# GpSimd in written order through the first tiles, and the side work of a factorization rearranged

## The chip, the cores and the metric

The program runs on one core of a Trainium2 chip. The metric is the device time of one execution in microseconds (us). Five engines run side by side and meet only at semaphores: TensorE (PE, with its weight loads shown as PEld), VectorE (DVE), ScalarE (ACT), GpSimd (POOL) and SyncE (SP), which issues the DMAs. A run has the time of the whole execution; the profile of one execution has a span, from its first to its last instruction.

## The reference

The function is a rotation of the tokens in a 64-dimensional subspace, followed by one transformer block that is modulated by a condition. All data are float32; 8 sequences of 512 tokens with 576 features.

```python
U, _ = jnp.linalg.qr(P)                      # P is 576 x 64
v = silu(cond) @ W.T + b                     # 8 x 2016
A = zeros(8, 64, 64).at[:, iu, ju].set(v).at[:, ju, iu].set(-v)
R = expm(A)                                  # 8 rotations, 64 x 64
z = x @ U
x = x + (z @ R - z) @ U.T

ada = silu(cond) @ ada_w + ada_b             # 8 x 3456, six parts of 576
shift_a, scale_a, gate_a, shift_m, scale_m, gate_m = split(ada, 6)
x = x + gate_a * attention(modulate(layernorm(x), shift_a, scale_a))
x = x + gate_m * mlp(modulate(layernorm(x), shift_m, scale_m))
```

The attention is between the 16 heads of one token, not between tokens: per token a 16 x 16 softmax over heads of 36 features. The MLP has 2304 hidden features and an exact GELU.

## The kernel before

The kernel has a preparation (lines 150 to 679) and a main part (from line 681).

**Preparation.** A Householder QR of P runs in 64 written steps, `qr_step(j, ...)` at line 259. One step is a chain: two small matmuls on PE (`rp` at line 262, `dp` at line 270), some ten small DVE instructions, two ACT instructions, and the DVE products of the next column (`column_products`). Beside it the generator `beside` (line 497) hands out work, one piece a step, called by `next(side, None)` after step j from j = 2 on. Its pieces are, in order:

- `ada_columns(g)`, nine groups of 384 columns of the modulation, each five PE products (line 352) accumulated in PSUM; six of the groups first, four products a step;
- `skew_entries(g)`, eight groups of the entries of A, five products of 252 columns each (line 385), four a step; then `skew_rows` sends them through DRAM into the tile `au`;
- `modulation(v)`, ten tiny transposing matmuls (line 363) that turn a row of `ada` into the per-feature tile `mod`, interleaved with single products of the last three `ada` groups;
- `expm`, the exponential: au is masked on POOL, powers by `products` (line 409, sixteen 64 x 64 matmuls a call), a polynomial whose sums run on POOL (lines 442 to 463), and 19 squarings with two POOL additions each (line 493). A `yield True` leaves room for one more piece from `rest` in that step, a `yield False` does not.

After step 63 a tail (lines 548 to 679) inverts a triangular matrix by doubling, level by level (lines 595 to 607), and builds `gz`, `u` and `ut`, with which the tokens are rotated; `normed` (line 130) prepares the layer norm of the first tile: two statistics on DVE, then the power -1/2 on POOL (line 140), then the scaling on DVE (line 141).

PE, DVE and ACT are in `tc.manual_schedule` during the preparation: their instructions run in the written order. POOL and SP are not in it before the change. For an engine outside of it a planner simulates the program and places instructions when they are ready in its simulation, with written order as the priority. In the main part all engines are planned this way.

**Main part.** Tokens go in tiles of 128. `rotation(b)` gives six pieces (project to z, rotate two tiles, and so again), `feature_major` (line 748) transposes normed tiles and applies `mod`, `qkv(b, i)` makes the attention inputs of a tile in four groups of ten PE matmuls, `attention(b, ts)` is DVE work of some sixteen 2.55 us instructions a tile. The work order is `units` (line 1081): the first two tiles alone (units 0 and 1, with `mlp_plain`), then pairs of tiles (with `mlp`). `mlp` computes the second layer by a seven-product scheme of 2 x 2 blocks that needs sums of weight blocks. `next_sums` (line 949), called ten times, makes them: call g first stores the sums of call g-1 to `comb_d` (SP, line 953), then loads block g into a tile `tt` (line 957, in a ring of three buffers shared with a part of the projection weights), and makes four sums on POOL (lines 960 to 963). Until the pairs begin, all nine sets must be made.

`mlp_plain` streams both MLP weights from HBM for one tile: `w1` (line 923, ring of four) and `w2` (line 980, ring of three).

Of the kernel before, what the change touches and what calls it, by code (L numbers as in the profile page):

```python
# [18 lines left out]
R = 64  # L19
# [29 lines left out]
def rotate_then_dit_block(  # L49
# [53 lines left out]
    def srows(c):  # L103
        return 65 if c == 4 else 128
# [42 lines left out]
    normed_x = {}  # L147


    engines = {mybir.EngineType.PE, mybir.EngineType.DVE, mybir.EngineType.Activation}  # L150
    sc = const.tile([128, NK, B], F32, tag="sc", name="sc")
    with tc.manual_schedule(engines=engines), tc.tile_pool(name="prep", bufs=1) as prep, tc.tile_pool(name="qrs", bufs=2) as qrs, tc.tile_pool(
        name="ada", bufs=4
# [271 lines left out]
        def expm(i1, i2, half):  # L425
# [35 lines left out]
                    nc.gpsimd.tensor_tensor(acc, acc, tp, ALU.add)  # L461
            nc.gpsimd.tensor_scalar(nan, nan, 0.0, 3e38, ALU.is_gt, ALU.mult)
            nc.gpsimd.tensor_scalar(nan, nan, 3e38, 0.0, ALU.mult, ALU.mult)
            for _ in range(5):
                yield True
            for name in ("c", "n"):
                lo, hi, tp = parts[name]
# [26 lines left out]
                yield False  # L494
            nc.gpsimd.tensor_tensor(fmi, f, nan.unsqueeze(2).to_broadcast([128, B // 2, R]), ALU.add)

        def beside():
            yield
            yield
            yield from paced(4, [ada_columns(g) for g in range(6)])  # L500
            yield from paced(4, [skew_entries(g) for g in range(8)])
            skew_rows()
            rest = paced(1, [ada_columns(g) for g in range(6, 9)])
            for v in (0, 1, 3):
                modulation(v)
                next(rest)
                yield
            for free in expm(*eyes):
                if free:
                    next(rest, None)  # L510
                yield
            for _ in rest:
                yield
            modulation(4)
            yield

        for g in range(4):
            load_ada(g)
        for g in range(4):
            cols = slice(g * NSKEW // 4, (g + 1) * NSKEW // 4)  # L520
            load_rows(wr[:, :, cols], rot_w[:, cols], 65)
        for g in (4, 5):
            load_ada(g)
        block_masks()
        first_xT = xin.tile([128, NK, 256], F32, tag="xT", name="xT_0_0")
# [4 lines left out]
        for j in range(R):  # L530
            t, done = qr_step(j, t, done)
            if j > 1:
                next(side, None)
            if j == 30:
                nc.sync.dma_start(out=first_xT, in_=x_t[0, :, :, 0:256].rearrange("c p s -> p c s"))
                nc.sync.dma_start(out=first_xt, in_=x[0, 0:128, :])
            if j == 8:
                load_rows(wqkv, qkv_w, 65)
                nc.sync.dma_start(out=b2, in_=fc2_b.to_broadcast([128, D]))
                for g in (6, 7, 8):  # L540
                    load_ada(g)
        for _ in side:
            pass

# [3 lines left out]
        if True:  # L548
# [32 lines left out]
            nc.tensor.matmul(vf_ps, lhsT=m[0:R, 0, :], rhs=fmi[0:R, 0, :], start=True, stop=True)  # L581
            vf = square("vf")
            nc.scalar.copy(vf, vf_ps)
            xps = ps_m.tile([R, R], F32, tag="m", name="xps")
            nc.tensor.matmul(xps, lhsT=y_, rhs=ident[0:R, 0:R], start=True, stop=True)
            nc.vector.scalar_tensor_tensor(ls[2], vv, rd, lower[2], ALU.mult, ALU.mult)
# [4 lines left out]
            for c, rows in enumerate(KROWS):  # L591
                ps = ps_ex.tile([R, 128], F32, tag="ex", name=f"vt_{c}")
                nc.tensor.transpose(ps[:, 0:rows], m[0:rows, c, :], ident[0:rows, 0:rows])
                nc.scalar.copy(vt[:, c * 128 : c * 128 + rows], ps[:, 0:rows])
            for c, s in enumerate(LEVELS[1:]):
                p1 = ps_qr.tile([R, R], F32, tag="dp", name=f"p1_{s}")
                nc.tensor.matmul(p1, lhsT=ls[s], rhs=x_, start=True, stop=True)
                vx_chunk(c)
                p1s = qrs.tile([R, R], F32, tag="p1s", name=f"p1s_{s}")
                nc.vector.tensor_copy(p1s, p1)  # L600
                p2t = ps_m.tile([R, R], F32, tag="m", name=f"p2t_{s}")
                nc.tensor.matmul(p2t, lhsT=p1s, rhs=y_, start=True, stop=True)
                if s < LEVELS[-1]:
                    p2 = ps_m.tile([R, R], F32, tag="m", name=f"p2_{s}")
                    nc.tensor.matmul(p2, lhsT=y_, rhs=p1s, start=True, stop=True)
                    nc.vector.tensor_tensor(x_, x_, p2, ALU.subtract)
                nc.vector.tensor_tensor(y_, y_, p2t, ALU.subtract)

            vxs = prep.tile([R, 128], F32, tag="vxs", name="vxs")
            nc.scalar.copy(vxs, vx)  # L610

# [44 lines left out]
            for n in range(2):  # L656
                cols = slice(n * HALF, (n + 1) * HALF)
                ps = ps_qr.tile([128, HALF], F32, tag="rp", name=f"first_rot_{n}")
                nc.tensor.matmul(ps, lhsT=first_zT, rhs=gz[0:R, cols], start=True, stop=True)
                nc.vector.tensor_tensor(first_xt[:, cols], first_xt[:, cols], ps, ALU.add)  # L660
                for c in (2 * n, 2 * n + 1):
                    u_rows(c, KROWS[c])
            nc.sync.dma_start(out=xr_d[0][0:128, :], in_=first_xt)
            normed_x[0, 0] = [normed(first_xt, "a0_0")]
            u_rows(4, KROWS[4])
            nc.vector.tensor_tensor(u[0:R, 0, 0:R], u[0:R, 0, 0:R], ident[0:R, 0:R], ALU.add)
# [81 lines left out]
    def feature_major(b, half):  # L748

        if b not in hTs:  # L750
            hTs[b] = big.tile([128, NK, S], F32, tag="hT", name=f"hT_{b}")
        hT = hTs[b]

        pair = normed_x.pop((b, half))
        first = half * 256 + (256 - len(pair) * 128 if b == 0 and half == 0 and turned else 0)
        turned.add((b, half))
        tokens = slice(first, first + len(pair) * 128)
        for c in range(NK):
            rows = srows(c)
            ps = ps_mm.tile([128, 2, 128], F32, tag="mm", name=f"htr_{b}_{half}_{c}")  # L760
            for t in range(len(pair)):
                nc.tensor.transpose(ps[:, t, :], pair[t][:, c * 128 : (c + 1) * 128], ident)
            nc.scalar.activation(
                hT[0:rows, c, tokens],
                ps[0:rows].rearrange("p t s -> p (t s)")[:, 0 : len(pair) * 128],
                AF.Identity,
                bias=mod[0:rows, 0, c, b : b + 1],
                scale=mod[0:rows, 1, c, b : b + 1],
            )

    toks = {}

# [312 lines left out]
            piece()  # L1085

    first = rotation(0)
    now(first[:1])
    feature_major(0, 0)
    now(qkv(0, 0))  # L1090
    now(first[2:3])
    feature_major(0, 0)
    next_sums()
    now(first[3:])
    next_sums()
    now(qkv(0, 1))
    feature_major(0, 1)
    attention(0, (0,))
    next_sums()
    now(qkv(0, 2))  # L1100
    gate_a = gate_m = gb2 = None
    for k, (b, ts) in enumerate(units):
        if ts[0] == 0:
            gate_a, gate_m = gate_rows(0, b), gate_rows(1, b)
            gb2 = big.tile([128, D], F32, tag="gb2", name=f"gb2_{b}")
            nc.gpsimd.tensor_tensor(gb2, gate_m, b2, ALU.mult)

        pr = Projection(b, ts, gate_a)
        if k == 2:
            next_sums()  # L1110
        if k == 0:
            q = qkv(0, 3)
        elif k == 1 or k + 1 == len(units):
            q = []
        else:
            nb, nts = units[k + 1]
            q = qkv(nb, nts[0]) + qkv(nb, nts[1])
        if len(ts) == 1:
            now(q[:3])
            pr.turn(0)  # L1120
# [92 lines left out]
```

## Time and profile before

| | us |
|---|---|
| median of 3 runs | 2202.04 |
| lowest to highest | 2199.09 to 2203.98 |
| the profiled execution, as a run | 2199.16 |
| its span | 2197.1 |
| PE busy | 2094.7 |
| DVE busy | 1797.5 |
| POOL busy | 691.1 |

The difference of 2.06 us between run and span lies around the instructions. PE is busy 95% of the span; most of the 5% lies in the first 460 us, which are the preparation and the two single tiles. In the profile a row of the timeline has start, length, engine, line, operation, output and inputs, shapes, and the number of merged instructions; a float32 matmul appears as two records.

### The profile page before, as it was taken

What the parts mean: (1) busy time and instruction counts of PE and PEld (TensorE: products, weight loads), DVE (VectorE), ACT (ScalarE), POOL (GpSimd) and SP (SyncE); (2) the same over time, 40 slices, a digit from 0 to 9 for tenths busy, and PEclk for the clock granted to TensorE, in tenths of its full rate; (3) what the DMA queues carried; (4) which work ended last, traced back from release to release, by engine and by line L of the source; (5) the groups of instructions that cost most, each with busy time, mean ns of one, the idle gap of its engine ahead of it and who ended that gap; (6) DMA issues with size and microseconds to landing.
All of it is one profiled execution on the core that took longest, in us unless ns stands there. A gap on an engine that the chain in (4) does not pass through costs nothing.

```text
span 2197.1 us, 26306 instructions
## 1 busy us (share of the span) xinstructions
PE 2094.7 (95%) x9609; PEld 1567.4 (71%) x9609; DVE 1797.5 (82%) x2450; ACT 389.7 (18%) x831; POOL 691.1 (31%) x882
## 2 busy tenths in 40 slices
PE   7897788899999999999999999999999999999998
PEld 3467446767777777868686868777776868686877
DVE  8998399899986979888896979697978888797930
ACT  2223121121021112111111112111211122111110
POOL 2144301003333333423241424243332334142422
PEclk9755699999999999999999999999999999999999
DMA  9103326845756473827374556546473737373753
GB/s 306 58 2 113 105 80 183 271 152 149 218 173 185 134 200 129 238 92 214 110 246 125 173 156 200 160 154 180 161 225 98 220 112 213 105 217 110 215 172 122
DMA packets 214291, 355.55 MB, mean 162 GB/s; under 512 B 82670, under 2 KB 101563, under 8 KB 214164
## 3 DMA queue, kind: packets, MB, share of 16 engines
q1 hardware_dynamic: 214164, 353.88, 53.0%
q8 instruction: 77, 1.26, 0.2%
q14 instruction: 50, 0.41, 0.1%
HBM read 321.43 MB, written 32.39 MB: 161 GB/s over the span
## 4 chain that ended last, share of the span: by engine, by line
PE 56%; DVE 23%; issue 12%; DMA 5%; POOL 3%; ACT 1%; SPq 1%; POOLq 0%; DVEq 0%; ACTq 0%
PE fc L926 23%; PE fc L1032 7%; DVE pv L831 5%; PE qkvp L784 5%; PE fc L1037 5%; DVE att L837 4%; DVE sc L815 4%; DVE qk L809 2%; PE fc L1034 2%; PE p L1047 2%; PE zps L725 2%; DMA out<-x 1%; PE rot L733 1%; PE dp L270 1%; DMA gate<-gates_d 1%
## 5 line engine op out<-in xcount | busy, mean ns | idle before, releaser
L926 PE MATMUL fc<-h2T,w 128*128 128x256 f32 (+3 forms) x3060 | 657.5, 368 | 1.4 <-ACT h2T L902 1.3
L926 PEld LDWEIGHTS fc<-h2T,w 128*128 128x128 f32 (+1 forms) x3060 | 550.1, 191 | 75.4 <-ACT h2T L902 6.5
L784 PE MATMUL qkvp<-wqkv,hT 128*128 128x432 f32 (+1 forms) x1280 | 478.6, 527 | 1.8 <-DVE pt L883 1.1
L809 DVE TENSOR_TENSOR qk<-qkv 128x2304 f32<-128x2304 f32 x128 | 330.2, 2580 | 124.4 <-ACT qkv L791 121.9
L784 PEld LDWEIGHTS qkvp<-wqkv,hT 128*128 128x128 f32 (+1 forms) x1280 | 239.7, 190 | 204.2 <-issue 195.4
L831 DVE TENSOR_TENSOR pv<-sc,qkv 128x2304 f32<-128x2304 f32 x128 | 330.1, 2579 | 3.2
L837 DVE TENSOR_REDUCE att<-pv 128x144 f32<-128x2304 f32 x128 | 326.6, 2551 | 3.2
L815 DVE TENSOR_REDUCE sc<-qk 128x64 f32<-128x2304 f32 x128 | 326.4, 2550 | 2.9
L1017 POOL TENSOR_TENSOR ss<-gt 128x128 f32<-128x128 f32 x135 | 143.0, 1060 | 579.5 <-ACT gt L934 579.5
L934 ACT ACTIVATE gt<-fc 128x512 f32<-128x512 f32 (+1 forms) x153 | 87.5, 572 | 716.9 <-PE fc L926 716.7
L791 ACT COPY qkv<-qkvp 128x432 f32<-128x432 f32 x128 | 66.3, 518 | 546.0 <-PE qkvp L784 545.9
L1037 PEld LDWEIGHTS fc<-wt,ss 128*128 128x128 f32 x1080 | 150.5, 190 | 14.2
L1037 PE MATMUL fc<-wt,ss 128*128 128x144 f32 x1080 | 154.4, 286 | 0.0
L1032 PE MATMUL fc<-wq,gt 128*128 128x288 f32 x540 | 153.0, 405 | 0.0
L140 POOL TENSOR_TENSOR rstd_m<-rstd_m,mhalf 128x1 f32<-128x1 f32 x32 | 19.8, 618 | 337.2 <-DVE rstd_m L139 337.2
L1063 DVE TENSOR_TENSOR u<-u,fc 128x288 f32<-128x288 f32 x15 | 6.8, 454 | 135.0 <-ACT u L1062 135.0
L1032 PEld LDWEIGHTS fc<-wq,gt 128*128 128x128 f32 x540 | 100.8, 189 | 21.3
L942 POOL TENSOR_TENSOR x<-x,mt 128x288 f32<-128x288 f32 x64 | 53.0, 829 | 183.0 <-DVE mt L941 183.0
L881 PE MATMUL pj<-w2q_p,aT 128*128 128x288 f32 x384 | 105.5, 411 | 3.9 <-DVE pt L883 1.8
L1019 POOL TENSOR_TENSOR ss<-gt,ss 128x128 f32<-128x128 f32 x135 | 101.8, 754 | 10.6
L1020 POOL TENSOR_TENSOR s<-gt 128x128 f32<-128x128 f32 x135 | 92.9, 688 | 0.0
L881 PEld LDWEIGHTS pj<-w2q_p,aT 128*128 128x128 f32 x384 | 70.0, 189 | 30.5 <-issue 7.1
(255 smaller groups left out, 2356.6 us busy)
## 6 DMA issues: line engine op xcount, KB each, us to landing
w<-in_fc_w SPq DMA_DIRECT2D x306, 320.0 KB, 3.5
wt<-comb_d SPq DMA_DIRECT2D x135, 432.0 KB, 5.2
wq<-in_fc_q SPq DMA_DIRECT2D x135, 432.0 KB, 3.3
w2q_p<-in_proj_w SPq DMA_DIRECT2D x34, 432.0 KB, 4.4
w<-in_fc_w SPq DMA_DIRECT2D x36, 288.0 KB, 3.8
xT<-in_x_t SPq DMA_DIRECT2D x16, 640.0 KB, 7.2
w2t_p<-in_proj_w SPq DMA_DIRECT2D x34, 288.0 KB, 5.1
xt<-in_x SPq DMA_DIRECT2D x32, 288.0 KB, 5.3
```

Of the source, the lines that this page charges most:

```text
L784: nc.tensor.matmul(ps, lhsT=hT[0:k, c, i * 128 : (i + 1) * 128], rhs=wqkv[0:k, c, n * N : (n + 1) * N], start=c == 0, stop=c == NK - 1,)
L809: nc.vector.tensor_tensor(pr, q[:, c * HC : (c + 1) * HC].unsqueeze(2).to_broadcast([128, HC, H, DH]), k.unsqueeze(1).to_broadcast([128, H ...
L815: nc.vector.tensor_reduce(sc2[:, t, c * HC : (c + 1) * HC, :], pr, AX.X, ALU.add)
L831: nc.vector.tensor_tensor(pr, sc2[:, t, c * HC : (c + 1) * HC, :].unsqueeze(2).to_broadcast([128, HC, DH, H]), v.unsqueeze(1).to_broadcast ...
L837: nc.vector.tensor_reduce(att[:, c * HC : (c + 1) * HC, :], pr, AX.X, ALU.add)
L881: nc.tensor.matmul(ps, lhsT=aT[0:k, c, :], rhs=w, start=c == 0, stop=c == NK - 1)
L926: nc.tensor.matmul(ps[:, k], lhsT=w1[0:n, c, :], rhs=h2T[0:n, c, 0 : NU * 128], start=c == 0, stop=c == NK - 1,)
L1017: nc.gpsimd.tensor_tensor(ss[:, 0], gt[:, 0, 1], gt[:, 1, 1], ALU.add)
L1019: nc.gpsimd.tensor_tensor(ss[:, 2], gt[:, 1, 0], ss[:, 1], ALU.subtract)
L1020: nc.gpsimd.tensor_tensor(s3s[g], gt[:, 0, 0], gt[:, 0, 1], ALU.subtract)
L1032: nc.tensor.matmul(p[k], lhsT=whole[k][0], rhs=whole[k][1], start=g == 0, stop=stop)
L1037: nc.tensor.matmul(bank[:, side], lhsT=lhs, rhs=rhs[:, n * QUARTER : (n + 1) * QUARTER], start=False, stop=stop, skip_group_check=True,)
```

## The change

POOL joins the manual schedule of the preparation, and a second manual schedule holds POOL alone from the first rotation until unit 2 begins. In `beside` the skew entries come first, four products a step; then a new generator `modulations` gives all nine groups of `ada` and the four modulations, three items a step: four steps alone, then in the `True` steps of `expm`, which has one `yield True` less. Weights for the skew entries are loaded first, and those of `ada` group g + 4 when group g is done. In the tail the products `vx_chunk` move to another place in each level, `vxs` is copied earlier, and the addition of the identity to `u` comes inside the loop over n. `feature_major` transposes up to four chunks of a single tile into one PSUM buffer before ScalarE reads them. The calls of `next_sums` are placed anew: one after the six pieces of the first rotation, two after the first attention, one before the MLP of unit 0 and two in it (g = 2 and 6), one before the MLP of unit 1 and two in it (g = 0 and 6), and the last in unit 2. There are still ten.

```diff
-    engines = {mybir.EngineType.PE, mybir.EngineType.DVE, mybir.EngineType.Activation}
+    engines = {mybir.EngineType.PE, mybir.EngineType.DVE, mybir.EngineType.Activation, mybir.EngineType.Pool}
...
-            for _ in range(5):
+            for _ in range(4):
                 yield True
...
+        def modulations():
+            for g in range(9):
+                yield from ada_columns(g)
+                if g + 4 < 9:
+                    load_ada(g + 4)
+                v = {1: 0, 2: 1, 5: 3, 7: 4}.get(g)
+                if v is not None:
+                    modulation(v)
+                    yield
+
         def beside():
             yield
             yield
-            yield from paced(4, [ada_columns(g) for g in range(6)])
             yield from paced(4, [skew_entries(g) for g in range(8)])
             skew_rows()
-            rest = paced(1, [ada_columns(g) for g in range(6, 9)])
-            for v in (0, 1, 3):
-                modulation(v)
+            rest = paced(3, [modulations()])
+            for _ in range(4):
                 next(rest)
                 yield
             for free in expm(*eyes):
...
             for _ in rest:
                 yield
-            modulation(4)
-            yield
-
-        for g in range(4):
-            load_ada(g)
+
         for g in range(4):
             cols = slice(g * NSKEW // 4, (g + 1) * NSKEW // 4)
             load_rows(wr[:, :, cols], rot_w[:, cols], 65)
-        for g in (4, 5):
+        for g in range(4):
             load_ada(g)
...
-                for g in (6, 7, 8):
-                    load_ada(g)
...
+            vxs = prep.tile([R, 128], F32, tag="vxs", name="vxs")
...
-            for c, s in enumerate(LEVELS[1:]):
+            vx_chunk(0)
+            for c, s in enumerate(LEVELS[1:], 1):
                 p1 = ps_qr.tile([R, R], F32, tag="dp", name=f"p1_{s}")
                 nc.tensor.matmul(p1, lhsT=ls[s], rhs=x_, start=True, stop=True)
-                vx_chunk(c)
                 p1s = qrs.tile([R, R], F32, tag="p1s", name=f"p1s_{s}")
                 nc.vector.tensor_copy(p1s, p1)
+                if s == LEVELS[-1]:
+                    nc.scalar.copy(vxs, vx)
...
                     nc.tensor.matmul(p2, lhsT=y_, rhs=p1s, start=True, stop=True)
+                    vx_chunk(c)
                     nc.vector.tensor_tensor(x_, x_, p2, ALU.subtract)
...
                     u_rows(c, KROWS[c])
+                if n == 0:
+                    nc.vector.tensor_tensor(u[0:R, 0, 0:R], u[0:R, 0, 0:R], ident[0:R, 0:R], ALU.add)
             nc.sync.dma_start(out=xr_d[0][0:128, :], in_=first_xt)
             normed_x[0, 0] = [normed(first_xt, "a0_0")]
             u_rows(4, KROWS[4])
-            nc.vector.tensor_tensor(u[0:R, 0, 0:R], u[0:R, 0, 0:R], ident[0:R, 0:R], ALU.add)
...
-        for c in range(NK):
-            rows = srows(c)
-            ps = ps_mm.tile([128, 2, 128], F32, tag="mm", name=f"htr_{b}_{half}_{c}")
...
+        at_once = 4 if len(pair) == 1 else 1
+        for first_c in range(0, NK, at_once):
+            cs = range(first_c, min(first_c + at_once, NK))
+            ps = ps_mm.tile([128, 4, 128], F32, tag="mm", name=f"htr_{b}_{half}_{first_c}")
+            for c in cs:
+                for t in range(len(pair)):
+                    at = (c - first_c) * len(pair) + t
+                    nc.tensor.transpose(ps[:, at, :], pair[t][:, c * 128 : (c + 1) * 128], ident)
+            for c in cs:
...
     first = rotation(0)
+    in_order = ctx.enter_context(ExitStack())
+    in_order.enter_context(tc.manual_schedule(engines={mybir.EngineType.Pool}))
     now(first[:1])
     feature_major(0, 0)
     now(qkv(0, 0))
     now(first[2:3])
     feature_major(0, 0)
-    next_sums()
     now(first[3:])
     next_sums()
     now(qkv(0, 1))
     feature_major(0, 1)
     attention(0, (0,))
+    next_sums()
     next_sums()
...
         if k == 2:
+            in_order.close()
             next_sums()
...
         if k == 0:
-            aside = {g: next_sums for g in (1, 3, 5, 7)}
+            aside = {g: next_sums for g in (2, 6)}
+        if k == 1:
+            aside |= {0: next_sums, 6: next_sums}
```

More of the change, by code (lines that the diff above doesn't have):

```diff
@@ L605, in rotate_then_dit_block @@
                     nc.tensor.matmul(p2, lhsT=y_, rhs=p1s, start=True, stop=True)
+                    vx_chunk(c)
                     nc.vector.tensor_tensor(x_, x_, p2, ALU.subtract)
                 nc.vector.tensor_tensor(y_, y_, p2t, ALU.subtract)
-            vxs = prep.tile([R, 128], F32, tag="vxs", name="vxs")
-            nc.scalar.copy(vxs, vx)
             w1_ps = ps_m.tile([R, R], F32, tag="m", name="w1_ps")
@@ L757, in feature_major @@
         tokens = slice(first, first + len(pair) * 128)
-        for c in range(NK):
-            rows = srows(c)
-            ps = ps_mm.tile([128, 2, 128], F32, tag="mm", name=f"htr_{b}_{half}_{c}")
[L761 to L769, printed above, removed]
+        at_once = 4 if len(pair) == 1 else 1
[7 more added lines that the diff above has]
+            for c in cs:
+                rows = srows(c)
+                at = (c - first_c) * len(pair)
+                nc.scalar.activation(
+                    hT[0:rows, c, tokens],
+                    ps[0:rows, at : at + len(pair)].rearrange("p t s -> p (t s)"),
+                    AF.Identity,
+                    bias=mod[0:rows, 0, c, b : b + 1],
+                    scale=mod[0:rows, 1, c, b : b + 1],
+                )
     toks = {}
```

## The prediction

> **What bounds the kernel now.** I read the page first, then the busy time of the engines stage by stage, then the waits of PE, then the timeline around the few stages where PE is not full.
>
> ```profile
> span 2197.1 us, 26306 instructions
> PE 2094.7 (95%) x9609; PEld 1567.4 (71%) x9609; DVE 1797.5 (82%) x2450; ACT 389.7 (18%) x831; POOL 691.1 (31%) x882
> ...
> PE   7897788899999999999999999999999999999998
> ...
> PEclk9755699999999999999999999999999999999999
> ```
>
> PE is the bound from the ninth slice on. Before it PE is neither full nor at full clock: what can be won lies there.
>
> ```profile
> 139.86:195.22 55.36, 54.62 (x668) 50.81 (x669) 53.18 (x310) 21.82 (x74) 25.33 (x36) 0.50 0.01 2
> 242.78:289.13 46.35, 30.13 (x82) 16.91 (x83) 25.28 (x23) 8.06 (x17) 15.81 (x14) 0.73 0.36 122
> 353.17:460.00 106.83, 97.52 (x586) 81.02 (x587) 94.42 (x81) 22.47 (x44) 6.99 (x9) 0.98 0.88 268
> 460.00:2197.00 1737.00, 1713.60 (x7505) 1308.99 (x7504) 1413.54 (x1173) 286.07 (x523) 583.00 (x693) 1.00 0.55 166
> ```
>
> Columns: stretch and length, busy us of PE, PEld, DVE, ACT, POOL, granted clock, DMA share, GB/s. The 19 squarings (139.86 to 195.22) take 2.91 us a step. The first rotation (242.78 to 289.13) leaves PE idle for 16 us. The two single tiles (353 to 460) run the DMA engines at 88%. After 460 us PE is 98.7% busy and the change touches nothing, so what is won or lost before 460 is the result.
>
> ```profile
> PE over L453 <- POOL ns L442: 3.3, 1, 3.3
> ...
> PE htr L762 <- DVE xm L141: 14.1, 1, 14.1
> PE fc L989 <- DMA w<-in_fc_w: 6.2, 8, 1.9
> ...
> PE zps L725 <- DVE u L666: 2.0, 1, 2.0
> ```
>
> Three of these waits end at POOL, once by way of DVE: it was doing something less urgent.
>
> **The change part by part.** The starts of QR steps are those of `rp` (line 262) in the timeline of PE: step 4 at 20.57, 5 at 26.59, 14 at 56.66, 31 at 118.01, 38 at 139.86, 57 at 195.22, 63 at 212.93. Where PE is not late a step lasts what DVE needs (its floor): 3.31 at step 13, 3.12 at 20, 2.98 near 33, 2.31 at 62.
>
> ```profile
> 22.32 4.34 PE L352 MATMUL ada<-aw,sc 128*8 128x384 f32 x8
> 30.64 2.75 PE L352 MATMUL ada<-aw,sc 128*8 128x384 f32 x8
> 89.95 1.45 PE L352 MATMUL ada<-aw,sc 128*8 128x384 f32 x2
> ...
> 58.02 1.87 PE L385 MATMUL skew<-wr,sc 128*8 128x252 f32 x8
> ```
>
> Two records are one product: 0.69 us at full clock (2.75/4), 1.4 at half.
>
> *Step 4, skew first.* The first four products warm the clock. Four `ada` took 4.34: about 4.6 records at 0.69 and the rest at 0.34, so some 3.2 us cold. Four skew products by the same rule: 6.7 records at 0.47, the rest at 0.23, 3.45. **-0.9.** Their first quarter of weights, now first in SP's queue, has 17 us to land (1.1 MB at 340 GB/s: 3.4).
>
> *Steps 5 to 13.* Four `ada` (2.75) made these PE-bound: 30.07. Four skew (1.87) leave them DVE-bound, nine floors near 3.40: 30.6. **+0.5.**
>
> *Steps 14 to 30.* Before: 61.35, of which 2.8 are two cold steps with a modulation (22, 23), 1.6 two more late ones, 4.2 the wait of `over`. There POOL ran seven polynomial instructions ahead of the tiny `ns` (issued at 109.68, its input ready at 105.5). In written order `ns` comes first and that wait goes; then DVE's reduction (105.11) is what POOL awaits, and seventeen polynomial instructions of 0.8 (14 us) are queued behind it, due five steps (16 us) later, two of them moved here from the kernel's start. After: floors of 52.4 (17 steps, mean 3.08). PE has 0.35 + 0.35 + 2.07 for three products, 2.77, hidden under the floor; with a modulation (1.26 warm at 80.36) instead of a product, or powers (0.65), it is over the floor, by 0.1, 0.8, 0.3, 0.7, 0.35, 0.3 and 1.0 in seven steps: 3.5. Add 1.0 for skew DMAs that nine `t` loads on SP (line 958, 7.7 us of issue) may now delay. The clock: three products stream 2.07 in a step of 3.2, more than the 1.87 that kept full clock in steps 12 to 20. The Trainium skill ("TensorE: Matmul & The Clock Gate", "HAM oscillation") says that a PE gap of over 3.4 us re-throttles. Step 27 has no product, a gap of some 4.2 us with only 64 x 64 matmuls, which held no clock in the squarings. By the row nothing is lost; by the rule step 28 runs cold at 4.14 for its products, about +2.2. I take 1.5, since such small matmuls run without raising 0.50. Sum 58.4, **-3.0.**
>
> *Steps 31 to 62.* The squarings now sit at 31 to 49. Seven meet the floor of about 3.1, twelve keep 2.91: 56.6. Then thirteen steps have no side work but one `ada` product in step 50: mean floor 2.52, 32.8. I read that floor from steps 58 and 62 (2.60, 2.31), since 59 to 61 are stretched to 3.39 by the weight sums on POOL, as the squarings are by its additions:
>
> ```profile
> 176.03 0.67 DVE L299 TENSOR_TENSOR m<-m,dg 128x1 f32<-128x1 f32 x1
> ...
> 211.65 0.15 DVE L299 TENSOR_TENSOR m<-m,dg 128x1 f32<-128x1 f32 x1
> ```
>
> The same instruction, beside POOL and without it. 89.4 against 94.92: **-5.5.** The QR makes **-8.9**.
>
> *Tail.* One `vx` product, 0.62, goes in front of the levels; the four others leave the gap before `p2t` (0.2 each) for that before the next `p1` (0.2 each): **+0.4**. `u` is complete before `ut`, so `zps` starts at about 240.9 and not 242.78: **-1.9**. With POOL in written order the power at 241.11 no longer waits behind a memset that waited for `ut`; its scaling then ends in time for the transposes.
>
> *Transposes of a single tile.* From 244.84 to the first `qkvp` at 247.71 five transposes alternate with ScalarE. Four at once: 4 x 0.36, a step of ScalarE 0.46, and a hop: 2.05. **-0.8**, and **-0.6** at the second, followed by `zps`.
>
> *The power of the second tile.*
>
> ```profile
> 272.95 0.14 DVE L139 TENSOR_SCALAR rstd_a<-mv_a 128x1 f32<-128x1 f32 x1
> 273.55 2.98 POOL L961 TENSOR_TENSOR t<-tt,t 128x288 f32<-128x288 f32 x1
> 278.23 0.55 POOL L140 TENSOR_TENSOR rstd_a<-rstd_a,mhalf 128x1 f32<-128x1 f32 x1
> 278.82 0.58 DVE L141 TENSOR_SCALAR xm<-xt,mv_a,rstd_a 128x576 f32<-128x576 f32 x1 [2.93 <-POOL rstd_a L140]
> 279.45 0.69 PE L762 MATMUL htr<-ident,xm 128*128 128x128 f32 x2 [14.06 <-DVE xm L141]
> ```
>
> The power was ready at 273.09 and started 5.1 us later, behind sums. But DVE has a 2.8 us product from 273.07 to 275.88 in front of the scaling: that is late next. Only DVE's own wait of 2.93 goes: **-2.9**, not 14.1. At 348.30 the same holds for unit 0's power: DVE is busy until 350.27, so freeing POOL brings nothing there.
>
> *The sums, later.* Eight of nine sets were loaded by 269, when DMA was nearly idle. The ring of three lets sets 0 to 2 load early again; 3 to 7 now come with units 0 and 1. Each moves 0.44 MB in and 0.44 out: 4.4 MB at 305 GB/s (268 over its share of 0.88) is 14.5 us, where the slack is 12% of 107, 13 us. Nothing if it fits in gaps, 14.5 if never. Queued behind a `comb_d` store on SP are the weight loads of the MLP; behind sets 6 and 7 on POOL is the power of the next rotation, due only at g = 7. I take a quarter: **+3.7.** Twelve sums also move beside the first attention. The skill ("SBUF — State Buffer", the section on its two sides) says that the loser of the port shared by DVE and POOL blocks for the whole other instruction: 0.79 for each of 12, over 9 us. Rows say less: a product beside sums took 2.96 (at 260.99) and 2.81, against 2.55, since most sums fit beside a one-input reduction. Three sets at 0.4: **+1.0** with rounding up.
>
> Sum: -8.9 + 0.4 - 1.9 - 0.8 - 0.6 - 2.9 + 3.7 + 1.0 = **-10.0**. The profiled execution took 2199.16 (span 2197.1 and 2.06 around it), 2.9 below the median of 2202.04. It would be 2189.2, and the median **2192.0**.
>
> **The rivals.**
> *A, slower: stores of sums block the weight stream.* SP issues in order. A `comb_d` store that awaits its sums (landing wait of 4.6 to 6.3, then 3.4 of sums) holds the `w1` and `w2` loads behind it, and PE has four `w1` tiles, two passes of 4.2 us, in hand. At 5 us for each of sets 3 to 7 it is 25: with the gains of 14.7 kept, 2202 - 14.7 + 26 = 2213. It decides from 14 us on. For it: PE already waits 6.2 for these weights at a DMA share of 0.88. Against: the planner places SP's instructions with the POOL order known, and stores 0 to 2 fall where DMA is idle.
> *B, slower: the clock stays at half in steps 18 to 30.* Products of 1.4 three a step make PE 1.2 + 4.14 + 0.5, 2.6 over the floor: thirteen steps, 34 us, 2226. Against: one cold step of such products re-warmed PE at 22.32.
> *C, little: the QR gains half.* If POOL's share of the port keeps DVE slow in steps 14 to 37 and the floor after 50 is 2.8, the QR brings 3 to 4 and the sum is -4: 2198. The short form, that POOL's written order changes nothing because the planner already did so, is excluded by the rows of `ns` and the power.
> Better than forecast, 2182, if the moved DMAs all fit and the planner also moves the second tile's scaling ahead of attention.
>
> **How the numbers follow.** Forecast (2184 to 2197, the better end within it) 0.60; A 0.15; B 0.05; C 0.20. A change under 0.2% (4.4 us) can't be told from none. Faster: 0.60 and 0.13 of C, 0.73. Same: 0.07 of C and 0.02 of A, 0.09. Slower: 0.13 of A and B, 0.18. The range goes from 2180 (all DMA cost gone and 2 more) to 2208, into A, leaving out its far end and B.
>
> **What would show it.** Right: step 14 near 56, 31 near 114, 63 near 204; no wait of `over` on `ns`; steps after 50 near 2.5; `ada` pairs at 0.69 in steps 14 to 26; `htr` waiting 11 rather than 14; `zps` without its wait on `u`. Wrong: `ada` pairs at 1.4 through the exponential (B); PE's wait on `w` well over 6.2 + 4, with SP's queue waiting for `tt` (A); steps after 50 at 2.9 (C).

## The result and the profile after

The kernel after takes 2204.36 us (median of 20 runs, 2199.71 to 2208.84), the kernel before beside it 2200.17 (20 runs, 2197.70 to 2204.92). The ratio is 1.0017, interval 1.0010 to 1.0023: slower by 0.17%. The forecast was 2192.0, faster by 0.45%. The profiled execution has a span of 2200.2 against 2197.1.

The page of the kernel after, span, busy times, and the rows of PE and of its granted clock:

```profile
span 2200.2 us, 26294 instructions
...
PE 2085.2 (95%) x9609; PEld 1562.6 (71%) x9609; DVE 1795.9 (82%) x2450; ACT 390.0 (18%) x831; POOL 703.2 (32%) x882
...
PE   6896797899999999999999999999999999999998
...
PEclk9955698999999999999999999999999999999999
```

PE is busy 9.5 us less than before for the same 9609 instructions, and yet the span is longer: PE waits more. From the ninth slice on the two rows have the same digits as before. So the answer lies again before 460 us, and the starts of single instructions tell it. They are read from the timelines of PE in both traces, in us from the start of the span:

| start of | before | after | after less before |
|---|---|---|---|
| QR step 14 | 56.66 | 55.05 | -1.6 |
| QR step 31 | 118.01 | 118.30 | +0.3 |
| QR step 63 | 212.93 | 207.11 | -5.8 |
| first `zps` (end of the tail) | 242.78 | 235.32 | -7.5 |
| second tile's `htr` | 279.45 | 268.82 | -10.6 |
| the `qkvp` behind it | 289.13 | 279.88 | -9.3 |
| first `fc` of unit 0 | 353.17 | 345.31 | -7.9 |
| first `qkvp` after unit 1's MLP | 456.02 | 461.05 | +5.0 |
| end of the span | 2197.1 | 2200.2 | +3.1 |

At the first `fc` of unit 0 the kernel after is ahead by 7.9 us. Unit 0 and unit 1, the two single tiles, lose 12.9. The same stretches in the busy times of the engines (length, busy us of PE, PEld, DVE, ACT, POOL, granted clock, DMA share, GB/s), kernel after:

```profile
55.05:118.30 63.25, 57.51 (x310) 26.28 (x311) 57.87 (x314) 15.55 (x59) 21.21 (x28) 0.89 0.25 74
118.30:207.11 88.81, 68.95 (x723) 61.94 (x723) 82.73 (x513) 28.41 (x102) 26.02 (x37) 0.53 0.13 45
345.31:461.05 115.74, 98.56 (x576) 82.58 (x577) 91.93 (x80) 22.52 (x44) 32.53 (x33) 0.92 0.83 264
461.05:2200.00 1738.95, 1716.30 (x7515) 1310.57 (x7513) 1416.08 (x1174) 286.33 (x523) 583.91 (x693) 1.00 0.58 167
```

The first row is QR steps 14 to 30: the clock is at 0.89, not at 1. The third is the two single tiles, 115.74 long. Here are the same two tiles in the kernel before, and then ten microseconds around their start in the kernel after:

```profile
353.17:456.02 102.85, 94.28 (x576) 79.22 (x577) 90.47 (x80) 22.47 (x44) 6.99 (x9) 0.98 0.88 267
```

```profile
340.00:350.00 10.00, 6.25 (x30) 5.58 (x31) 9.93 (x5) 3.47 (x7) 7.38 (x5) 0.54 0.01 2
```

Before, 102.85 us at 267 GB/s are 27.5 MB. Now it is 30.6 MB, in more time and at a lower share of the DMA engines: there is more to carry, and from 340 to 350 us almost nothing is carried (DMA share 0.01). The 12.9 us are of two kinds. PE waits longer for `w1` and `w2` (14.3 us in the kernel after, 10.0 and 4.3 in the rows below; 5.5 before), and its 576 records take 98.56 us in place of 94.28, at a granted clock of 0.92 in place of 0.98. What PE waits for from 200 to 480 us (total, times, longest):

```profile
PE htr L771 <- DVE xm L141: 10.9, 1, 10.9
PE fc L938 <- DMA w<-in_fc_w: 10.0, 2, 8.0
...
PE fc L1001 <- DMA w<-in_fc_w: 4.3, 5, 1.5
```

and what SP's own queue waits for, from 320 to 470 us:

```profile
SPq L965 <- POOL tt L975: 26.2, 4, 15.0
```

`htr` waits 10.9 where it waited 14.1, as forecast. The wait of 8.0 for a `w1` tile is new. `SPq L965` is the `comb_d` store: four of them held the queue for 26.2 us in all, against one and 5.8 before. Here are the two rows of SP's timeline, and the row of PE that ends the wait:

```profile
352.25 5.89 SPq L965 DMA_DIRECT2D comb_d<-tt  x2
358.24 2.01 SPq L935 DMA_DIRECT2D w<-in_fc_w  x4
```

```profile
361.75 4.58 PE L938 MATMUL fc<-h2T,w 128*128 128x128 f32 x20 [7.96 <-DMA w<-in_fc_w]
```

Two stores stand directly ahead of four `w1` loads. The stores wait for sums that GpSimd makes from 346.6 on, and the loads, for which buffers are free, are issued only at 358.24. PE has used the tiles in hand by 353.8 and stands still to 361.75; its next twenty records then take 4.58, where twenty take 2.39 later on (368.11). That is rival A of the prediction, in one place, at a third of its price.

### The profile page after: what moved, and what is told of

The parts are those of the page before. It is cut to its first block, busy times and chain, and to the rows that moved or that the text cites. A ratio compares the mean times of both kernels' runs of the same rounds, so it can differ in the third digit from the quotient of the medians.

```text
span 2200.2 us, 26294 instructions
## 1 busy us (share of the span) xinstructions
PE 2085.2 (95%) x9609; PEld 1562.6 (71%) x9609; DVE 1795.9 (82%) x2450; ACT 390.0 (18%) x831; POOL 703.2 (32%) x882
## 3 DMA queue, kind: packets, MB, share of 16 engines
q8 instruction: 77, 1.26, 0.2%
## 4 chain that ended last, share of the span: by engine, by line
PE 57%; DVE 19%; issue 13%; DMA 5%; POOL 3%; ACT 1%; SPq 1%; POOLq 0%; DVEq 0%; ACTq 0%
PE fc L938 24%; PE fc L1044 7%; PE fc L1049 5%; PE qkvp L796 5%; DVE sc L827 4%; DVE pv L843 3%; DVE att L849 3%; PE fc L1046 2%; PE p L1059 2%; DVE qk L821 2%; DMA out<-x 2%; PE zps L731 2%; DMA w<-in_fc_w 1%; PE fc L1001 1%; PE rot L739 1%
## 5 line engine op out<-in xcount | busy, mean ns | idle before, releaser
L1031 POOL TENSOR_TENSOR ss<-gt,ss 128x128 f32<-128x128 f32 x135 | 99.8, 740 | 10.6
L893 PEld LDWEIGHTS pj<-w2q_p,aT 128*128 128x128 f32 x384 | 70.0, 189 | 29.8 <-issue 6.2
```

Source lines behind the costliest of these rows:

```text
L893: nc.tensor.matmul(ps, lhsT=aT[0:k, c, :], rhs=w, start=c == 0, stop=c == NK - 1)
L1031: nc.gpsimd.tensor_tensor(ss[:, 2], gt[:, 1, 0], ss[:, 1], ALU.subtract)
```

## The experiments

Theory, after the traces were compared: the loss has two places. In QR steps 14 to 30 PE falls to half clock, above all behind step 27, which has no `ada` products (C). In the two single tiles the sets' stores block SP's queue (A) and their bytes compete with the weights (D). The rivals: GpSimd's sums slow VectorE through their shared port (P); the tiles are bound by their own weight transfers, so that an earlier start is given back there whatever is done (L). The letters are those of the expectations below; this C is the prediction's rival B in fewer steps, not its rival C, and the block (A) is called theory S in e1 to e3.

**e1: the stores leave SP's queue.** The kernel after, with one line changed:

```diff
-            nc.sync.dma_start(out=comb_d[g - 1], in_=made_of[g - 1])
+            nc.gpsimd.dma_start(out=comb_d[g - 1], in_=made_of[g - 1])
```

> The changed kernel with one edit: the nine stores of the weight sums (comb_d) are issued by GpSimd behind the sums themselves, not by SyncE. Orders of the other engines hardly move. Theory S (in the changed kernel a store in SyncE's queue waits for sums that written order made late, and the weight loads of unit 0's MLP stand behind it): PE's 8.0 us wait at the first load of unit 0's MLP goes, and with it some 8 us: 2196, against 2204 of the changed kernel. Rival D (the DMA engines are simply full with 4.4 MB more in units 0 and 1): the bytes are the same, so 2204 and the waits on weights stay at about 14 us in total. Rival P (the port that GpSimd shares with VectorE stretches the sums to 3 us and VectorE's products with them): 2204 or more.

Measured: 2201.49 us, ratio to before 0.9999 (0.9990 to 1.0008). SP and PE in unit 0:

```profile
349.57 2.49 SPq L935 DMA_DIRECT2D w<-in_fc_w  x4
```

```profile
345.04 6.66 PE L938 MATMUL fc<-h2T,w 128*128 128x128 f32 x40 [0.22 <-ACT h2T L914]
```

The loads go out 8.7 us earlier, the 8 us wait is gone, and unit 0's part (first `fc` to unit 1's first `pj`) takes 47.77 in place of 55.65. So the queue caused the wait. But of the 7.9 us only 4.0 reach the end of unit 1: its part takes 3.9 more (windows of e1, the two tiles together):

```profile
345.04:456.77 111.73, 96.73 (x576) 79.88 (x577) 95.92 (x81) 22.47 (x44) 37.79 (x40) 0.97 0.90 287
```

111.73 x 287 GB/s is 32.1 MB, 4.6 more than before, and the DMA engines are at 90%. With the block gone PE still waits 12.5 us for weights, in twelve short waits.

**e2 and e3: the change in two halves.** e2 has the new preparation (and the new transposes) with GpSimd free behind it and `next_sums` at the old places; e3 has the old preparation with the new main part.

> Only the part up to the first rotation is changed (side work of the QR, GpSimd in written order in the preparation, the tail, the transposes of single tiles); main part with the calls of the weight sums and the planner's GpSimd order as before. The order list shows that the planner puts six sets of sums right behind the last squaring's additions, so beside QR steps 51 to 62. Theory S: the preparation's gain of 5.8 to 7.4 us is kept but for some 3 us of those steps that the sums slow: 2195 to 2197, and PE's waits on weights are as before, 6 us. Rival L (whatever the preparation gains is lost later, since VectorE or the DMA engines set the pace of the single tiles): 2200.

```diff
     first = rotation(0)
-    in_order = ctx.enter_context(ExitStack())
-    in_order.enter_context(tc.manual_schedule(engines={mybir.EngineType.Pool}))
...
-            aside = {g: next_sums for g in (2, 6)}
-        if k == 1:
-            aside |= {0: next_sums, 6: next_sums}
+            aside = {g: next_sums for g in (1, 3, 5, 7)}
```

> Only the part from the first rotation on is changed (GpSimd in written order there, the new places of the weight sums); preparation as before. Theory S: unit 0's MLP loses the 8 to 10 us that the changed kernel loses there, units 1 and 2 some 3; the sums no longer slow QR steps 58 to 61 (2.7 back) and the scaling of the second tile comes 2.9 earlier: 2204 to 2208. Rival L: the loss is that of the changed kernel alone, made by the earlier start of its main part: 2200.

```diff
-    engines = {mybir.EngineType.PE, mybir.EngineType.DVE, mybir.EngineType.Activation, mybir.EngineType.Pool}
+    engines = {mybir.EngineType.PE, mybir.EngineType.DVE, mybir.EngineType.Activation}
...
-            rest = paced(3, [modulations()])
+            rest = paced(1, [ada_columns(g) for g in range(6, 9)])
```

Measured: e2 2199.01, ratio 0.9987 (0.9980 to 0.9995); e3 2207.16, ratio 1.0021 (1.0015 to 1.0027). The preparation is worth -0.13%, the new main part +0.21%; together +0.08%, where the whole change has +0.17% (0.10 to 0.23). In e2 the freed planner puts sums beside QR steps 52 to 62 (in the kernel before, beside 58 to 62), and step 63 starts at 213.62: the QR gain is gone, and the time is nearer to L's 2200 than to the 2195 to 2197 of the theory. So the gain of steps 31 to 62 and the loss in the tiles belong to the same decision, the sums' place. In e3 the two tiles take 116.1, as in the kernel after. In e2 they take 107.8, with the sums' traffic outside of them: 5 more than in the kernel before.

**e4: no modulations beside the exponential.** The four modulations are postponed to steps behind the squarings:

```diff
                 if v is not None:
-                    modulation(v)
-                    yield
+                    later.append(v)
...
             for _ in rest:
                 yield
+            for v in later:
+                modulation(v)
+                yield
```

> The changed kernel with one edit: the four modulations are not put between the ada products but into four steps after the squarings' side work. Theory C (in steps 17 to 30 the clock falls to half for a while after each modulation, and a step with three products at 1.4 us is PE-bound): the clock stays at full to step 27, steps 14 to 31 take 58 to 59 us and not 63.2; the kernel 2200. Rival T (the modulations only lengthen four PE-bound steps by what they take themselves): 2.2 us less, 61, and pairs of records at 1.4 us still appear: 2202.

Measured: 2204.99, ratio 1.0009 (1.0002 to 1.0015). Steps 14 to 30 took 62.0, against 63.25; both numbers expected, 58 to 59 and 61, were too low. The clock now stays at 1.00 to the end of step 27 and then falls to half; steps 28 and 29 take 5.9 and 5.8:

```profile
105.00:110.00 5.00, 4.55 (x9) 1.22 (x9) 3.58 (x23) 0.91 (x3) 0.00 (x0) 0.52 0.01 2
110.00:115.00 5.00, 5.00 (x26) 2.44 (x26) 2.88 (x18) 0.81 (x3) 2.30 (x4) 0.50 0.00 0
```

So the modulations did bring the clock down in steps 18 and 25 of the kernel after, but the larger fall is another's, by the theory that of the step without products.

**e5: products in step 27 too.** e4 with one word changed, at the step of `hi` products:

```diff
-            yield False
+            yield True
             yield True
```

> This is the version with the four modulations moved behind the exponential (e4), with one thing more: step 27, which had no ada products, gets three. Theory C (the half clock of steps 28 to 30 comes from the step without products): the products of steps 28 and 29 take 2.1 and not 3.8 to 4.0, steps 14 to 31 take 59 to 59.5 and not 62.0 (step 27 itself grows by 0.8, two steps shrink by 2), and the total falls by some 2.5, to 2202.5, if the rest of the kernel keeps it. Rival F (the steps are bound by VectorE beside GpSimd's polynomial, and the clock is lost for another reason): the products of step 28 stay at 3.8 or more, 61.5 to 62.5, total 2205.

Measured: steps 14 to 30 took 58.73; total 2201.92, ratio 0.9996 (0.9988 to 1.0004), 0.13% or 2.9 us below e4. The timeline of PE around steps 27 and 28, first of the kernel after, then of e5:

```profile
102.62 0.68 PE L409 MATMUL hic<-ex_hic,ex_s 64*64 64x64 f32 x16
103.14 0.63 PE L409 MATMUL hin<-ex_hin,ex_s 64*64 64x64 f32 x16
104.86 0.41 PE L262 MATMUL rp<-m,ident 128*128 128x36 f32 x2 [1.09 <-DVE m L325]
106.23 0.38 PE L270 MATMUL dp<-t,ones 128*128 128x36 f32 x2 [0.96 <-DVE av L294]
106.55 3.79 PE L352 MATMUL ada<-aw,sc 128*8 128x384 f32 x6
```

```profile
103.47 0.63 PE L409 MATMUL hin<-ex_hin,ex_s 64*64 64x64 f32 x16
104.03 2.10 PE L352 MATMUL ada<-aw,sc 65*8 65x384 f32 x6
106.07 0.41 PE L262 MATMUL rp<-m,ident 128*128 128x36 f32 x2
106.57 0.38 PE L270 MATMUL dp<-t,ones 128*128 128x36 f32 x2
106.88 2.10 PE L352 MATMUL ada<-aw,sc 128*8 128x384 f32 x6
```

Six records are three products. With products in step 27 those of step 28 take 2.10, without them 3.79 (4.01 in e4), and e5's clock from 105 to 110 us is 1.00:

```profile
105.00:110.00 5.00, 3.75 (x28) 1.89 (x28) 4.82 (x32) 1.62 (x6) 0.43 (x1) 1.00 0.01 2
```

Theory C is shown for step 27: one step in which PE has only 64 x 64 matmuls, `rp` and `dp` is enough. The edit adds no product, it brings three forward, so that steps 29 and 30 have none. There the clock falls too (`dp` takes 0.61 from 113.45 on), but no product is left behind it that could be late.

**e6: the sets' bytes taken out of the two tiles.** The kernel after, but sets 3 to 8 have neither load nor store there; GpSimd does four operations of the same size at the same places on data that is already in SBUF. These sets' sums are left out, and their products use unsummed weights.

```diff
-        if g < NP:
+        if 3 <= g < NP:
+            for _ in range(4):
+                nc.gpsimd.tensor_tensor(t3[:, g], t3[:, g], t3[:, g], ALU.subtract)
+        elif g < NP:
```

> The kernel after, with GpSimd's four operations for each of the weight sets 3 to 8 at the same places and of the same size, but on data that is already there; their loads and stores are left out of the two single tiles (the sums of these sets are left out, the products with them use unsummed weights, copied in steps 30 to 40 of the QR). Theory D (the loss is the sets' traffic: stores ahead of weight loads in SP's queue, and bytes): from the first fc of unit 0 to the first qkvp after unit 1's MLP it takes 102 to 105, against 115.8 in the kernel after and 102.9 before; total 2191 to 2194. Rival P (the loss is GpSimd's work beside VectorE's, through their shared port, and the late normalisation): 112 or more, total 2200 to 2204. Rival L (the two tiles are bound by their own weight transfers, and an earlier start is given back there): 107 to 110, total 2196 to 2199.

Measured: 2194.46, ratio 0.9970 (0.9956 to 0.9985). In the profiled execution the two tiles took 108.65, against 115.74: 7 of the 12.9 us went with the sets' traffic, as block and as bytes together, and 5.8 stayed, within what L had said. The ratios give the traffic more: 0.9970 against 1.0017 is some 10 us. The profiled execution was the slowest of the seven, 2201.87 us (it spent 67.5 us in steps 14 to 30, see e11).

**e9: and GpSimd's work as well.** As e6, without the four operations:

```diff
-        if 3 <= g < NP:
-            for _ in range(4):
-                nc.gpsimd.tensor_tensor(t3[:, g], t3[:, g], t3[:, g], ALU.subtract)
-        elif g < NP:
+        if g < 3:
```

> As e6_no_bytes, with GpSimd's operations for the weight sets 3 to 8 left out too (so these sets have neither loads, nor stores, nor sums; the products with them use unsummed weights). What is left of the units' loss in e6 (108.65 from the first fc of unit 0 to the first qkvp after unit 1's MLP, 5.7 over the kernel before) is either GpSimd's work, theory P: then 102 to 104 here, and the total some 4 below e6, near 2190; or the tiles' own weight transfers meeting an earlier start, or the spread from one execution to the next, theory L: then 107 to 110 again, and the total within 2 of e6, 2192 to 2196.

Measured: 2193.67, ratio 0.9966 (0.9953 to 0.9979); the two tiles took 108.15:

```profile
345.93:454.08 108.15, 97.10 (x576) 81.46 (x577) 90.67 (x80) 22.48 (x44) 7.00 (x9) 0.96 0.84 254
```

GpSimd is busy 7.00 in place of e6's 29.82, and the tiles gain 0.5: P, if there is anything in it, is below what these runs resolve. 108.15 x 254 GB/s is 27.5 MB, the amount of before, at 254 and not 267 GB/s. Of the 5.3 us over the kernel before, 2.8 are slower matmuls (97.10 busy for 94.28) and 2.6 longer waits for weights (8.1 for 5.5). What makes them isn't settled; the sums don't, for e2 has the 5 us too. L as worded (an earlier start is given back) does not order the runs: those without set traffic in the tiles took 107.8 (e2, start 350.8), 104.7 (e7, 347.8), 108.15 (e9, 345.9), 112.3 (e8, 341.8) and 105.8 (e10, 340.3). e7 and e8 have the same main part and are 7.6 apart, so a difference of a few microseconds between two single profiles of this stretch says little.

**e7: the sums where GpSimd and the DMA engines idle.** Five sets between the end of the QR and the first power, held back by a one-element copy per partition that needs the last column; two between the powers of the first and the second tile, the last two beside the first attention; none in the single tiles' MLPs.

```diff
+            nc.scalar.copy(held[:, 0:1], vmax[:, R - 1 : R])
...
+    nc.gpsimd.tensor_copy(held[:, 1:2], held[:, 0:1])
...
+    for _ in range(5):
+        next_sums()
```

> The kernel after, with the weight sums between the end of the QR and the first power (five sets, held back until the QR's last column by one small copy), two sets between the first and the second tile's power, two more before the second attention: none in the two single tiles. Theory D: the QR keeps its gain (step 63 near 207), the two tiles take 102 to 105, total 2191 to 2194, better than both kernels. Rival P: sums beside the levels and the attention slow VectorE there; the first qkvp is later than 240.3 by 2 or more and the second htr later than 268.8 by 3 or more, total 2197 to 2200. Rival L: 107 to 110 for the two tiles, total 2196 to 2199.

Measured: 2196.09, ratio 0.9973 (0.9964 to 0.9982), 2 us above the range expected. The two tiles took 104.68, and steps 31 to 62 took 88.3, so the QR kept its gain. Step 63 started at 211.08, because in this execution steps 14 to 30 took 65.9 and steps 5 to 13 took 31.2 (63.25 and 29.8 in the kernel after). From step 63 to the first `qkvp` it was 33.6 against 33.2: the sums beside the tail cost little.

**e8 and e10: both cures.** e8 is e7 with e5's two edits. e10 makes the last two sets, too, ahead of the second tile's power:

```diff
     now(qkv(0, 0))
-    next_sums()
-    next_sums()
+    for _ in range(4):
+        next_sums()
     now(first[2:3])
```

> e7 and e5 in one: sums between QR and first power, modulations behind the exponential, products in step 27. Theories C and D: the gains add, 2189 to 2192 (e7 less 2 to 3). Rival L (an earlier start is given back in the two single tiles): the start of unit 0 is 2 to 3 earlier than in e7 but the end is the same within 1. Rival F: as e7 within 1, with steps 14 to 31 at 61.5 or more.

> As e8_early_clock, with the last two weight sets made between the first and the second tile's power too, so that none lies beside the first attention. If the port shared by VectorE and GpSimd costs there what the rows say (two products of 3.0 in place of 2.56), fc of unit 0 starts 0.9 earlier relative to the first qkvp, and the total falls by 1 or less, to 2188.5; if the two sets come late (their ring waits for stores) the second tile's power is delayed and the total rises by 2 to 4.

Measured: e8 2189.38, ratio 0.9946 (0.9935 to 0.9958); e10 2189.87, ratio 0.9949 (0.9936 to 0.9961). The gains of e5 and e7 add up, and both kernels beat the one before by 0.5%; that the last two sets' place makes no difference leaves the cost of the port beside the first attention below what these runs resolve. Windows of e10, QR steps 14 to 30 and the two tiles:

```profile
55.48:114.16 58.68, 47.82 (x272) 21.04 (x272) 57.04 (x308) 14.44 (x52) 21.19 (x28) 0.97 0.27 81
340.30:446.09 105.79, 95.81 (x576) 80.50 (x577) 90.68 (x80) 22.50 (x44) 7.00 (x9) 0.97 0.86 260
```

Against the kernel after: clock 0.97 in place of 0.89, and 58.68 for 63.25; POOL 7.00 for 32.53 and 105.79 for 115.74.

**e11: the kernel after again.**

> The kernel after once more, beside these. Same total as before within the spread, 2203 to 2206. Its profile tells what changes from one execution to another: if the clock in QR steps 14 to 30 is set by the written order alone, these steps take 63 to 63.5 again; if this order is at the edge of the clock's rule they take up to 68, as in the profiles of e6 and e7, which have the same preparation. The two single tiles: 114 to 117 if the loss there belongs to the kernel; further off if it is spread.

Measured: 2205.26, ratio 1.0020 (1.0013 to 1.0028), the same result. Steps 14 to 30 took 63.35, the two tiles 117.9, and SP's stores waited 26.3, with the longest 15.0 (26.2 and 15.0 in e3, e4 and e5 too): the block belongs to the kernel. The clock does not quite: with this same order on PE these steps took 63.25, 63.23 (e1), 63.22 (e2) and 63.35, but 67.5 (e6), 65.9 (e7) and 66.0 (e9). With e5's edits they took 58.73, 58.72 (e8) and 58.68 (e10).

## Why the prediction was wrong, step by step

| step of the sum | forecast | measured | |
|---|---|---|---|
| step 4 | -0.9 | -1.2 | right |
| steps 5 to 13 | +0.5 | -0.3 (to +1.1 in e5) | within the spread |
| steps 14 to 30 | -3.0 | +1.9 (to +6.2 in e6) | wrong, the clock |
| steps 31 to 62 | -5.5 | -6.1 | right |
| tail: `vx`, `zps` | -1.5 | -1.6 | right |
| transposes, first tile | -0.8 | 0.0 | wrong, small |
| second tile's power | -2.9 | -3.2 | right |
| transposes, second tile | -0.6 | +1.4 | wrong |
| first attention (port) | +1.0 | +1.4 | right in size, the reason not shown: e10, without sums there, has +0.8 |
| sums' transfers in units 0 and 1 | +3.7 | +12.9 | wrong, the largest |
| from 461 us on | 0 | -1.9 | 1739.2 for 1741.1; the other profiles have 1738.4 to 1741.3 |
| sum (span; -0.2 lies ahead of step 4) | -10.0 | +3.1 | |

**The sums' transfers.** This term decided the sign. "4.4 MB at 305 GB/s ... is 14.5 us, where the slack is 12% of 107, 13 us ... I take a quarter" took free share for free time. The bytes were nearly right (3.1 MB more in the kernel after, 4.6 in e1), the quarter was not. By the ratios, whose intervals do not overlap, the queue's block is worth 0.18%, 4 us (kernel after against e1), and the rest of the sets' traffic 0.29%, 6 us (e1 against e6): 10 of the 12.9. The single profiles give 4.0, then 3.6 down to e9, and 5.3 that stay over the kernel before. They are rougher: with the traffic and its stores on SP the two tiles took 114.5 to 117.9 in five profiles (after, e3, e4, e5, e11), without traffic 104.7 to 112.3 in six (e2, e6 to e10), and the 102.85 of before is one profile alone. The reason given against rival A, that "the planner places SP's instructions with the POOL order known", is refuted by the two rows at 352.25 and 358.24: it put two stores that wait in front of loads that could have gone. A named five places at 5 us; there was one, at 8. What stays without any set traffic, 3 us by the ratios and 5.3 by the profiles, is open.

**Steps 14 to 30.** The prediction had both readings of step 27: by the row nothing, by the Trainium skill ("TensorE: Matmul & The Clock Gate", "HAM oscillation") a cold step at +2.2, and took 1.5 for it. Step 28 did run cold: so the rule fits, if 64 x 64 matmuls count as a gap, which the prediction had assumed and e4 shows. e5 against e4 is 3.3, since step 29 runs cold too. The step that failed here is the one for the modulations: the prediction gave them their own time only and put their effect on the clock at nothing, since three products a step "stream 2.07 in a step of 3.2, more than the 1.87 that kept full clock". A modulation is five 8-column matmuls (ten records; the counts given above for lines 363 and 409 are of records, two to a matmul). They keep PE busy for 1.26, and the clock fell behind them: in step 18 the products took 3.38, in step 25 3.12, where 2.10 is full speed.

```profile
66.87 1.26 PE L363 MATMUL mod<-ident,ada_rows 8*128 8x8 f32 x10
...
70.03 3.38 PE L352 MATMUL ada<-aw,sc 128*8 128x384 f32 x6
```

That 58.7 of e5 is close to the 58.4 forecast is partly chance: e5 has no modulations over the floor, but VectorE's 308 instructions alone take 57.1 us there, 3.36 a step, where the forecast had a floor of 3.08 (before, 53.77 us, 3.16 a step).

**What was right.** `over` waits no more for `ns`. The thirteen steps from 50 on take 2.42 each on the mean (175.65 to 207.11), and steps 57 to 62, without sums beside them, 14.1 in place of 17.7; the tiny instruction of line 299 takes 0.15 there. `zps` no longer waits for `u` (that wait, too, had ended at GpSimd by way of VectorE: before, the addition to `u` stood behind the scaling that waited 2.62 for the power).

**The small ones.** The first tile's power, said to start before the memset, still stands behind it; the `xm` memsets belong to neither written order and wait for `ut`:

```profile
235.59 0.24 POOL L118 MEMSET xm<- 128x64 f32 x2 [58.71 <-PE ut L675]
235.79 0.57 POOL L140 TENSOR_TENSOR rstd_a<-rstd_a,mhalf 128x1 f32<-128x1 f32 x1
```

Four transposes into one PSUM buffer save PE's hops, but the ScalarE copies then start late and stand in one row: `htr` to `qkvp` takes 2.65 against 2.66 in the first tile (the 2.87 of the forecast was counted from the weight load at 244.84), and in the second `zps` starts 2.72 behind `htr` against 2.41, with a wait of 1.4 for `hT`, and runs at a lower clock (4.63 for 3.94, granted 0.50 for 0.60). The forecast had counted one ScalarE step.

Rivals B and C are refuted in their mechanism: the clock did fall, but in five to eight steps and not in thirteen, and the steps after 50 reached 2.4, not C's 2.8. Of C only the first half was seen, VectorE's longer time in steps 14 to 30. The time, 2204.4, fell between C's and A's figure.

## What to carry to other kernels

A transfer moved to where the DMA engines are at 88% is not hidden by the 12% left: move it to where they idle, and read the in-order queue's list for a store that waits ahead of loads that need not. Making work wait until it is due moved it into the busiest stretch; e10 kept the order's gain by placing the same sums in the gap behind the QR. Where small matmuls share a stretch with full-size products, let no step before the last product go without some: one such step cost 3.3 us, and bringing three products forward, by one word, mended it.

## What the runs showed of the hardware

PE being busy does not keep the clock. In the squarings PE was busy for 54.62 of 55.36 us, and the granted clock was 0.50. Behind step 27 of e4, with only 64 x 64 matmuls, `rp` and `dp`, it fell from 1.00 to 0.52, and behind a modulation of 8 columns three products took 3.38 in place of 2.10. One and the same order on PE took 63.2 to 67.5 us for the same 17 steps; in the three longer executions step 14 had started at 56.2 to 56.9, in the four shorter ones at 55.1 to 55.3. Nor does a wait tell the clock by its length: behind a wait of 2.56 for weights e7's twenty `fc` records took 2.39, behind one of 2.55 in e10 they took 4.01. The Trainium skill ("TensorE: Matmul & The Clock Gate", "What's actually happening") describes a free-running window of activity, which would make the phase matter; that is argued, not shown.

A one-column power on GpSimd took 2.87 us where it takes 0.55, most likely because VectorE's product of two SBUF operands had started 0.11 us before it (rows of VectorE and of GpSimd, kernel after):

```profile
265.18 2.56 DVE L821 TENSOR_TENSOR qk<-qkv 128x2304 f32<-128x2304 f32 x1
```

```profile
265.29 2.87 POOL L140 TENSOR_TENSOR rstd_a<-rstd_a,mhalf 128x1 f32<-128x1 f32 x1 [28.06 <-DVE rstd_a L139]
```

265.18 + 2.56 is 267.74; the power ends at 268.16, 0.42 behind it, most of its 0.55: it stood still for nearly the whole product, as the Trainium skill says of the port's loser ("SBUF — State Buffer", "SBUF: two separate sides"). The prediction had weighed the port for long sums only; here the loser is a 0.55 us instruction on the path, and the scaling behind it started 0.45 late. It cost little because VectorE itself was busy with that product.
